# Batched row scatters and reordered LayerNorm statistics in an attention and mixture-of-experts layer

## The chip, the cores and the metric

The kernel runs on one core of a Trainium2 chip. Such a core has five engines, each with an instruction queue of its own that it works off in order: TensorE (PE, matrix products), VectorE (DVE), ScalarE (ACT), GpSimd (POOL) and SyncE (SP, which here issues most DMA transfers). The metric is the device time of one execution in microseconds (us), lower being better.

## The reference

The input x has 32 sequences of 256 tokens with 128 features, 8,192 tokens in all. Everything is float32.

```python
mod = (_silu(c) @ wmod).reshape(32, 6, 1, -1)          # sa, ca, ga, sb, cb, gb
h = _layernorm(x) * (1 + ca) + sa
x = x + ga * attn(h)                                   # gated linear scan
h = _layernorm(x) * (1 + cb) + sb
x = x + gb * ffn(h)                                    # 8 experts, top 2

def attn(x):
    g = sigmoid(x @ Wg.T + bg)
    a = sigmoid(x @ Wd.T + bd)
    v = x @ Wv.T + bv
    return scan(h_t = a_t * h_{t-1} + (1 - a_t) * v_t) * g

def ffn(x):
    probs = softmax(x @ gate_w.T + gate_b)
    topk_vals, topk_idx = top_k(probs, 2)
    h = relu(einsum('nd,edh->neh', x, w1) + b1)        # hidden size 512
    y = einsum('neh,eho->neo', h, w2) + b2
    return sum over the two chosen experts of topk_vals * y
```

## The kernel before

**Supertiles.** The tokens are taken in 16 supertiles of 512 (four tiles of 128, T = 4). Each supertile goes through four steps:

- `a_norm` (L312): first LayerNorm. VectorE's `bn_stats` (L280) and `bn_aggr` (L282) give mean and variance, `rsqrt` (L284 to L308) a reciprocal root in some ten small VectorE steps (for the first three supertiles with a power on GpSimd), ScalarE writes the normalised tiles (L324).
- `a_mix`: transposes px (L337), gated projections pz (L346), the scan on VectorE (L365, L366).
- `a_res`: transposes po back (L374), the residual (L376), the statistics of the second LayerNorm and its normalised tiles xm (L382, ScalarE).
- `a_route` (L385): transposes ph, logits pl (L397), the rows to be routed, rw (L402, ScalarE), top 2 of 8 on VectorE, ranks among the tokens of the same expert by small matmuls pq (L423, L425), and from these the row numbers pi (L439, VectorE). Then the weights of the two choices are added to rw (L444), and the token numbers by GpSimd (L445). Each supertile has 8 scatters (4 tiles, 2 choices, L447): GpSimd sends 128 rows each with an indirect DMA into a DRAM buffer `reg`, in which each expert has a region of its own.

**Blocks.** The rows in `reg` are worked off in 71 blocks of 256 rows of one expert. After supertiles 2 to 8, 10 and 12 (TAKE) and after the last, `table` (L471) works out from the running counts which blocks are certainly full, and puts the expert and first row of each into a small table tb. The tables hold blocks 0 to 4 (supertile 2), then four each up to block 28 (supertiles 3 to 8), 29 to 36 (10), 37 to 44 (12) and 45 to 70 (15). After the last supertile `fills` (L522) pads what is left of each region.

A block goes through `b_load` (SyncE reads expert and row from tb, L535 and L536, loads 256 rows xr, 130 KB, L538, and the expert's first-layer weights ww, 514 KB, L544; ww has five buffers, loads run four blocks ahead), `b_in` (transposes pbx, L551), `b_up` (three products p per part, L566 to L568; bias and relu to hh, L572 and L574), and `b_down` (bias matmul pby L584, products L587, weighted copy yt on ScalarE L591, eight buffers, and two scatters of result rows by GpSimd into DRAM, yd L593). The three are staggered: in one `b_step`, block i enters, block i-1 is in `b_up`, block i-2 in `b_down`. When all rows of a supertile are there, `c_load` (L600) and `c_add` (L610) sum its two results and the residual and write the output.

**Order.** A hand-written order (HEAD, L31) opens the program; after that each round t runs a_norm of supertile t, a_mix of t-1, a_res of t-2 and a_route of t-3, with a `b_step` after most of the steps as soon as more than two blocks are ready (L677 to L735). The program order, with priorities (AHEAD) for the later steps, decides each engine's queue order.

**How scatters are sent now.** `a_route` doesn't issue its 8 scatters: it puts them on a list (`sending`). `drip` (L461) takes one or two of the list at a time, after each step and each `b_step`, and gives each scatter a wait on a ScalarE instruction of the step or block just emitted (the activations remembered under "last"). Blocks of a new table lie in `held` until the last scatter of that table's supertile has been emitted, and only then join `blocks`. In `b_load` each xr load carries explicit waits on the last 16 scatters, and its value loads are kept behind the load of the block before it.

Two further places matter: rw (L401) and pi (L438) have three buffers each, and `late_constants` (L218), called after round 3, prepares constants of the final sum (among them sT3, the transformed rows mr and the selector sel, L227 to L240).

Of the kernel before, what the change touches and what calls it, by code (L numbers as in the profile page):

```python
# [15 lines left out]
AX = mybir.AxisListType  # L16
WAIT = mybir.DependencyInfo(mybir.DependencyClass.Sync, mybir.DependencyReason.DATA)

# [13 lines left out]

LATE = 3

XE = 3
# [19 lines left out]
def adaln_moe(ctx: ExitStack, tc: tile.TileContext, x, Wg, bg, Wv, bv, Wd, bd,  # L55
# [164 lines left out]
    def late_constants():  # L220
        nc.vector.tensor_copy(b2s[:, 0], b2r)
        nc.vector.tensor_tensor(b2s[:, 1], b2r, b2s[:, 0], op=ALU.subtract)
        for h in range(2):
            nc.sync.dma_start(b2w[h:h + 1].bitcast(F32), b2s[:, h].bitcast(F32))


        sT3 = cp.tile([P, 3, NB], F32, name="sT3")  # L227
        nc.vector.tensor_copy(sT3, sT.unsqueeze(1).to_broadcast([P, 3, NB]))
        pr = psa.tile([P, 512], F32, tag="pq", name="pr")
        nc.tensor.matmul(pr[:N3, :D], sT3.rearrange("p a b -> p (a b)"), wm[:, 5 * D:], start=True, stop=True)  # L230
        mr = cp.tile([N3, D], F32, name="mr")
        guarded(mr, pr[:N3, :D], [N3, D], 1.0, "gr")
        nc.vector.tensor_copy(mr3, mr)
        for i in (1, 2, 2):
            w = slice(i * NB, (i + 1) * NB)
            nc.vector.tensor_tensor(mr[w], mr[w], mr3[w], op=ALU.subtract)
            nc.vector.tensor_copy(mr3[w], mr[w])

        nc.vector.tensor_tensor(sel, ident[:N3, 0:NB], ident[:N3, NB:2 * NB], op=ALU.add)
        nc.vector.tensor_tensor(sel, sel, ident[:N3, 2 * NB:N3], op=ALU.add)  # L240
# [34 lines left out]

    def stats(mv, src, name):
        n = src.shape[1]
        st = wk.tile([P, T, 6], F32, tag=f"st{name[0]}", name=f"st{name}")
        for j in range(n):
            nc.vector.bn_stats(st[:, j], src[:, j])  # L280
        for j in range(n):
            nc.vector.bn_aggr(mv[:, j], st[:, j])  # L282
# [27 lines left out]
    ln1 = {}  # L310

    def a_norm(s):  # L312
        g = LN1G.get(s, 0)
        if g:
            mv = wk.tile([P, g * T, 2], F32, tag=f"mva{g}", name=f"mva{s}")
            for i in range(g):
                stats(mv[:, i * T:(i + 1) * T], xa[:, s + i], f"a{s + i}")
            y, r = rsqrt(mv, f"a{s}", s)
            for i in range(g):
                ln1[s + i] = (y[:, i * T:(i + 1) * T], r[:, i * T:(i + 1) * T])  # L320
        y, r = ln1[s]
        xn = wk.tile([P, T, D], F32, tag="xn", name=f"xn{s}")
        for j in range(T):
            last = nc.scalar.activation(xn[:, j], xa[:, s, j], AF.Identity, scale=y[:, j], bias=r[:, j])  # L324
        return dict(s=s, xn=xn, last=last)

# [6 lines left out]
    def a_mix(a):  # L333
# [10 lines left out]
        for i in (2, 1, 0):  # L344
# [3 lines left out]
            if i == 2:  # L348
                ta = wk.tile([P, ST], F32, tag="ta", name=f"ta{s}")
                nc.scalar.activation(ta, z, AF.Tanh, scale=0.5, bias=hb[:, 2:3])  # L350
                aa = wk.tile([P, ST], F32, tag="aa", name=f"aa{s}")
                nc.scalar.activation(aa, ta, AF.Copy, scale=0.5, bias=0.5)
                for q in range(BPS):
                    w = slice(q * S, (q + 1) * S)
                    b = s * BPS + q
                    nc.vector.tensor_scalar(ta[:, w], ta[:, w], ngq[:, b:b + 1], gq[:, b:b + 1], op0=ALU.mult, op1=ALU.add)
            elif i == 1:
                nc.vector.scalar_tensor_tensor(ta, z, bvc, ta, op0=ALU.add, op1=ALU.mult)
            else:
                tg = wk.tile([P, ST], F32, tag="tg", name=f"tg{s}")  # L360
                a["last"] = nc.scalar.activation(tg, z, AF.Tanh, scale=0.5, bias=hb[:, 0:1])  # L361
        hs = wk.tile([P, ST], F32, tag="hs", name=f"hs{s}")
# [6 lines left out]
    def a_res(a):  # L369
# [11 lines left out]
        for j in range(T):  # L381
            a["last"] = nc.scalar.activation(xn[:, j], xt[:, j], AF.Identity, scale=y[:, j], bias=r[:, j])  # L382
        a["xn"] = xn

    def a_route(a, base):  # L385
# [13 lines left out]
        for j in range(T):  # L399
            nc.tensor.transpose(pb[:, j * P:(j + 1) * P], hT[:, j * P:(j + 1) * P], ident)  # L400
        rw = wk.tile([P, T, K, RW], F32, tag="rw", name=f"rw{s}", bufs=3)  # L401
        a["last"] = nc.scalar.activation(rw[:, :, :, 0:D], pb.rearrange("p (t d) -> p t d", d=D).unsqueeze(2).to_broadcast([P, T, K, D]), AF.Copy)  # L402
        lg = wk.tile([P, T, E], F32, tag="lg", name=f"lg{s}")
# [33 lines left out]
        nc.vector.tensor_reduce(pf, oh, axis=AX.X, op=ALU.add)  # L437
        pi = wk.tile([P, T * K], I32, tag="pi", name=f"pi{s}", bufs=3)  # L438
        nc.vector.tensor_copy(pi, pf.rearrange("p t k -> p (t k)"))  # L439
        sm = wk.tile([P, T], F32, tag="sm", name=f"sm{s}")  # L440
# [4 lines left out]
        nc.gpsimd.tensor_copy(rw[:, :, :, D + 1].bitcast(I32), dst[:, s * T:(s + 1) * T])  # L445
        def send(j, k):
            w = nc.gpsimd.indirect_dma_start(  # L447
                out=reg, out_offset=bass.IndirectOffsetOnAxis(ap=pi[:, j * K + k:j * K + k + 1], axis=0),
                in_=rw[:, j, k], in_offset=None)
            into_reg(w.ins, "scat")  # L450
            return w.ins

        sending.extend((s, send, j, k) for j in range(T) for k in range(K))
        return rk[:, T]


    sending = []
    sent = []
    held = []

    def drip(n, behind):  # L461
        for _ in range(min(n, len(sending))):
            s, send, j, k = sending.pop(0)
            w = send(j, k)
            tc.add_manual_dep(w, behind.ins.name, WAIT, reason="pace of the rows on their way out")
            sent.append(w)
            if not sending or sending[0][0] != s:
                while held and held[0][0] <= s:
                    blocks.extend(held.pop(0)[1])

# [59 lines left out]

    loaded = []

    def b_load(n, tb, i):
        with tc.issue_after(loaded[-1].ins) if loaded else nullcontext():
            e = nc.sync.value_load(tb[i:i + 1, 0:1], min_val=0, max_val=E - 1)  # L535
            r = nc.sync.value_load(tb[i:i + 1, 1:2], min_val=0, max_val=E * CAP)  # L536
        xr = bk.tile([P, NJ, RW], F32, tag="xr", name=f"xr{n}", bufs=YTB + 6)
        w = nc.sync.dma_start(xr, reg[bass.ds(r, BLK)].rearrange("(t p) d -> p t d", p=P))  # L538
        tc.add_to_no_dep_group("rows", w.ins)
        for x in sent[-2 * K * T:]:  # L540
            tc.add_manual_dep(w.ins, x.name, WAIT, reason="its rows")
        ww = bk.tile([P, WW], F32, tag="ww", name=f"ww{n}", bufs=5)
        b = dict(n=n, xr=xr, ww=ww, tb=tb, i=i)
        loaded.append(nc.sync.dma_start(ww, wd[bass.ds(e, 1)].rearrange("o p f -> p (o f)")))  # L544
        return b
# [11 lines left out]
    def b_up(b):  # L557
        n, xs, ww = b["n"], b["xs"], b["ww"]
        hh = bk.tile([P, NH, BLK], F32, tag="hh", name=f"hh{n}")
        for k0 in range(0, NH, 2):  # L560
# [8 lines left out]
            for k in (k0, k0 + 1):  # L569
# [3 lines left out]
                else:  # L573
                    w = nc.scalar.activation(hh[:, k], p1[:, k - k0], AF.Relu, bias=bias)  # L574
                    b.setdefault("last", w)
        b["hh"] = hh
# [56 lines left out]
    def b_step():  # L633
# [12 lines left out]
        if i >= 1 and flow[i - 1]:  # L646
            b_up(flow[i - 1])
            drip(1 if alive else 2, flow[i - 1]["last"])
        if i >= 2 and flow[i - 2]:
# [7 lines left out]
    slot = 0  # L657
    alive = True

# [24 lines left out]
    for t, todo in enumerate(steps):  # L684
        def step3(s):
            nonlocal base, done
            with tc.high_priority(AHEAD[3] * (s >= EARLY)):
                base = a_route(st[s], base)
                if s in CLS:
# [3 lines left out]
                    counts.append(b)  # L693
                nb = len(blocks) + sum(len(x) for _, x in held)
                if s in TAKE:
                    n = full(s) - nb
                    tb, done = table(s, counts[:1] * (s > CUT) + [base], done, n, False)
                    held.append((s, [(tb, q, []) for q in range(n)]))
                elif s == NS - 1:
                    n = touched(s) - nb  # L700
                    tb, done = table(NS, counts, done, n, True)
                    fills(base)
                    rest = [(tb, q, []) for q in range(n)]
                    held.append((s, rest))
                    z = 0
                    for c in CLS:
                        u = max(E, touched(c) - nb) if c == CUT else touched(c) - nb
                        rest[u - 1][2].extend(range(z, c + 1))
                        z = c + 1
# [13 lines left out]
        for i, s in todo:  # L723
            (step0, step1, step2, step3)[i](s)
            drip(2 if t < len(steps) - NS or len(sending) > K * T else 1, st[s]["last"])
            between()
# [4 lines left out]
        if t == LATE:  # L731
            late_constants()
    alive = False
    while len(flow) < len(blocks) + 2 or ended or adding:
        b_step()  # L735
    assert not sending and not held

# [27 lines left out]
```

## Time and profile before

| what | value |
|---|---|
| median of 14 runs | 544.82 us (542.92 to 549.79) |
| profiled execution, whole | 545.21 us |
| its span | 543.4 us |
| PE busy | 440.2 us (81% of the span) |
| PE weight load busy | 368.0 us (68%) |
| VectorE busy | 283.3 us (52%) |
| ScalarE busy | 288.3 us (53%) |
| GpSimd busy | 292.5 us (54%) |
| mean granted clock of PE | 0.87 |

The profile is of one execution. Busy time of PE includes matmuls that run at a lower granted clock, so a busy PE is not one at its best. Further places of the trace that are of use below:

| what | when (us) |
|---|---|
| row numbers pi of supertiles 0, 1, 2, 3 written (start of L439) | 46.3, 59.9, 64.5, 89.6 |
| pi of supertiles 8, 12, 15 | 193.2, 283.5, 344.2 |
| supertile 0's eight scatters | 47.70 to 57.97 |
| last scatter of supertile 15 starts | 406.6 |
| first block's transposes | 100.4 |
| rows out for blocks 31, 36, 41, 46 (yt) | 349.2, 377.9, 409.2, 432.8 |
| last block's rows out | 530.5 |

Indirect DMAs on GpSimd take 0.95 to 1.5 us each (L447: 128, 981 ns on the mean; L593: 142, 998 ns), with 0.30 us between one and the next when nothing else holds them.

### The profile page before, as it was taken

Reading aid. Unit: us, or ns where it says so; the run is one execution under the profiler, and the core shown is the slowest. Engines: PE = TensorE matmul, PEld = TensorE weight load, DVE = VectorE, ACT = ScalarE, POOL = GpSimd, SP = SyncE. Lnnn points to the kernel's source line nnn. Section 1 sums busy time; section 2 is a strip of 40 time slices with the busy share of each in tenths; the row PEclk is TensorE's granted clock in tenths of the full one; section 3 lists DMA queues with packets and bytes.
Section 4 is the critical chain, followed back from the end, with each engine's and each line's share of the span. In section 5 each row is a group of like instructions: output and inputs, shape, how many; then the busy total and the mean of one; then the engine's idle time right before and its main releaser. Section 6 shows DMA issues by size and latency. Waiting matters only on the chain.

```text
span 543.4 us, 11399 instructions
## 1 busy us (share of the span) xinstructions
PE 440.2 (81%) x2810; PEld 368.0 (68%) x2810; DVE 283.3 (52%) x1511; ACT 288.3 (53%) x726; POOL 292.5 (54%) x322
## 2 busy tenths in 40 slices
PE   5868557698797899879969797895967999989990
PEld 3335315576786778658768686784966999979980
DVE  6899899476572765547556532311110221344364
ACT  4777445657573667646555553333323556655650
POOL 4436653445656656655566665565665255545451
PEclk9875675698797979898979996899889899999997
DMA  7993110647163644444442664566417777999974
GB/s 212 330 313 154 45 40 20 193 122 219 46 191 100 180 129 136 108 133 131 135 111 71 188 170 118 167 173 188 139 46 205 208 226 217 274 330 312 317 216 128
DMA packets 81845, 91.52 MB, mean 168 GB/s; under 512 B 8577, under 2 KB 66408, under 8 KB 81782
## 3 DMA queue, kind: packets, MB, share of 16 engines
q1 hardware_dynamic: 73024, 73.84, 47.4%
q0 software_dynamic: 8704, 16.94, 9.1%
q8 instruction: 26, 0.43, 0.3%
q14 instruction: 37, 0.30, 0.2%
q10 hardware_dynamic: 54, 0.02, 0.0%
HBM read 64.24 MB, written 27.43 MB: 169 GB/s over the span
## 4 chain that ended last, share of the span: by engine, by line
PE 52%; DVE 13%; issue 9%; another core or an unknown queue 9%; ACT 8%; DMA 5%; SPq 2%; POOL 1%; ACTq 0%; POOLq 0%; DVEq 0%
PE pby L587 22%; PE p L566 5%; PE p L568 5%; PE p L567 5%; PE pz L346 4%; PE pby L584 4%; PE pbx L551 3%; ACT yt L591 2%; DMA yk<-yd 2%; ACT hh L574 1%; PE pl L397 1%; DVE sta L280 1%; DVE hs L365 1%; DMA xa<-in_L_attn_x_dram 1%
## 5 line engine op out<-in xcount | busy, mean ns | idle before, releaser
L593 POOL DMA_INDIRECT yd<-yt,xr x142 | 141.7, 998 | 134.3 <-ACT yt L591 96.8
L447 POOL DMA_INDIRECT reg<-rw,pi x128 | 125.6, 981 | 76.8 <-issue 37.1
L587 PE MATMUL pby<-wr,hh 128*128 x1136 | 164.8, 302 | 0.8 <-issue 0.7
L587 PEld LDWEIGHTS pby<-wr,hh 128*128 128x128 f32 x1136 | 149.5, 211 | 10.4 <-issue 2.0
L574 ACT ACTIVATE hh<-p,ww 128x256 f32<-128x256 f32 x231 | 95.8, 479 | 36.9 <-issue 10.9
L591 ACT ACTIVATE yt<-pby,xr 128x128 f32<-128x128 f32 x142 | 44.9, 364 | 132.4 <-PE pby L587 60.1
L554 DVE TENSOR_TENSOR xs<-pbx,xs 128x256 fp32r<-128x256 f32 x71 | 29.9, 421 | 133.4 <-ACT xs L553 99.6
L566 PE MATMUL p<-xs,ww 128*128 128x256 f32 x284 | 91.7, 324 | 8.6 <-DVE hh L572 4.3
L567 PE MATMUL p<-xs,ww 128*128 128x256 f32 x284 | 83.0, 293 | 0.5 <-issue 0.4
L568 PE MATMUL p<-xs,ww 128*128 128x256 f32 x284 | 83.0, 293 | 0.0
L346 PE MATMUL pz<-h,wT 128*128 128x512 f32 x96 | 60.5, 752 | 5.8 <-ACT tg L361 3.3
L566 PEld LDWEIGHTS p<-xs,ww 128*128 128x128 f32 x284 | 57.1, 202 | 11.7 <-DVE hh L572 5.6
L567 PEld LDWEIGHTS p<-xs,ww 128*128 128x128 f32 x284 | 57.2, 201 | 2.2 <-issue 2.0
L584 PE MATMUL pby<-b2w,ones_r 2*128 x71 | 28.2, 397 | 35.2 <-ACT yt L591 33.3
L568 PEld LDWEIGHTS p<-xs,ww 128*128 128x128 f32 x284 | 56.5, 199 | 0.2 <-issue 0.2
L584 PEld LDWEIGHTS pby<-b2w,ones_r 2*128 2x128 f32 x71 | 13.6, 191 | 52.3 <-ACT yt L591 39.2
L572 DVE TENSOR_SCALAR hh<-p,ww 128x256 f32<-128x256 f32 x53 | 25.4, 479 | 22.4 <-ACT hh L574 17.6
L346 PEld LDWEIGHTS pz<-h,wT 128*128 128x128 f32 x96 | 20.2, 241 | 22.3 <-issue 9.4
L551 PE MATMUL pbx<-ident,xr 128*128 128x128 f32 x142 | 30.3, 298 | 4.1 <-DMA xr<-reg 3.2
L553 ACT ACTIVATE xs<-pbx 128x256 fp32r<-128x256 f32 x71 | 27.4, 386 | 10.0 <-PE pbx L551 3.8
L324 ACT ACTIVATE xn<-xa,nra,nya 128x128 f32<-128x128 f32 x64 | 26.5, 498 | 8.4 <-DVE nra L307 8.4
L382 ACT ACTIVATE xm<-xa,nrb,nyb 128x128 f32<-128x128 f32 x64 | 26.4, 483 | 6.2 <-DVE nyb L306 3.6
(181 smaller groups left out, 591.9 us busy)
## 6 DMA issues: line engine op xcount, KB each, us to landing
ww<-wd SPq DMA_DIRECT2D x71, 514.0 KB
xr<-reg SPq DMA_DIRECT2D x71, 130.0 KB
yk<-yd SPq DMA_DIRECT2D x30, 256.0 KB
wd<-wh SPq DMA_DIRECT2D x8, 514.0 KB
xa<-in_L_attn_x_dram SPq DMA_DIRECT2D x16, 256.0 KB
out_dram<-ot SPq DMA_DIRECT2D x15, 256.0 KB
yd<-yt,xr POOLq DMA_INDIRECT x142
w1s<-in_L_ffn_w_dram SPq DMA_DIRECT2D x8, 256.0 KB
```

The lines of the kernel that those rows point to most:

```text
L346: nc.tensor.matmul(z, wT[:, i], h1, start=True, stop=True)
L447: w = nc.gpsimd.indirect_dma_start(out=reg, out_offset=bass.IndirectOffsetOnAxis(ap=pi[:, j * K + k:j * K + k + 1], axis=0), in_=rw[:, j, ...
L551: nc.tensor.transpose(px[:, j * P:(j + 1) * P], xr[:, j, 0:D], ident)
L554: nc.vector.tensor_tensor(xs[:, 1], px, xs[:, 0], op=ALU.subtract)
L566: nc.tensor.matmul(z, hi, xs[:, 0], start=True, stop=False)
L567: nc.tensor.matmul(z, hi, xs[:, 1], start=False, stop=False)
L568: nc.tensor.matmul(z, lo, xs[:, 0], start=False, stop=True)
L574: w = nc.scalar.activation(hh[:, k], p1[:, k - k0], AF.Relu, bias=bias)
L584: nc.tensor.matmul(py.rearrange("p (j d) -> p j d", d=D), ones_r, b2t, start=True, stop=False)
L587: nc.tensor.matmul(py[:, j * D:(j + 1) * D], hh[:, k, j * P:(j + 1) * P], we[:, k * D:(k + 1) * D], start=False, stop=(j == NJ - 1 and k = ...
L591: nc.scalar.activation(yt[:, j], py[:, j * D:(j + 1) * D], AF.Copy, scale=xr[:, j, D:D + 1])
L593: w = nc.gpsimd.indirect_dma_start(out=yd, out_offset=bass.IndirectOffsetOnAxis(ap=xr[:, j, D + 1:D + 2].bitcast(I32), axis=0), in_=yt[:, ...
```

## The change

The eight scatters of a supertile are issued together at the end of `a_route`. The list, `drip`, `held` and the ScalarE instructions remembered for them are gone, and a table's blocks join `blocks` as soon as the table is emitted. The loads of rows lose their explicit waits on the 16 scatters (the dependence of the load on the scatters into `reg`, by the groups that `into_reg` declares, stays), and the value loads lose their order behind the load of the block before. rw and pi go back from three buffers to the pool's two. The first-LayerNorm `bn_stats` get an order (same engine, no semaphore) behind the pi copy of the supertile that was routed last when they are emitted: those of supertile 3 behind pi of 0, of 4 behind pi of 1, and so on. The second half of `late_constants` becomes `later_constants`, called after round 8.

```diff
-WAIT = mybir.DependencyInfo(mybir.DependencyClass.Sync, mybir.DependencyReason.DATA)
+ORDER = mybir.DependencyInfo(mybir.DependencyClass.NoSync, mybir.DependencyReason.DATA)
+LATER = 8
...
+    def later_constants():
         sT3 = cp.tile([P, 3, NB], F32, name="sT3")
...
-    def stats(mv, src, name):
+    def stats(mv, src, name, behind=None):
...
-            nc.vector.bn_stats(st[:, j], src[:, j])
+            w = nc.vector.bn_stats(st[:, j], src[:, j])
+            if behind:
+                tc.add_manual_dep(w.ins, behind.name, ORDER, reason="not ahead of the supertiles that route")
...
-                stats(mv[:, i * T:(i + 1) * T], xa[:, s + i], f"a{s + i}")
+                stats(mv[:, i * T:(i + 1) * T], xa[:, s + i], f"a{s + i}", placed[-1] if placed else None)
...
-        rw = wk.tile([P, T, K, RW], F32, tag="rw", name=f"rw{s}", bufs=3)
+        rw = wk.tile([P, T, K, RW], F32, tag="rw", name=f"rw{s}")
...
-        pi = wk.tile([P, T * K], I32, tag="pi", name=f"pi{s}", bufs=3)
-        nc.vector.tensor_copy(pi, pf.rearrange("p t k -> p (t k)"))
+        pi = wk.tile([P, T * K], I32, tag="pi", name=f"pi{s}")
+        placed.append(nc.vector.tensor_copy(pi, pf.rearrange("p t k -> p (t k)")).ins)
...
-        sending.extend((s, send, j, k) for j in range(T) for k in range(K))
+        for j in range(T):
+            for k in range(K):
+                w = nc.gpsimd.indirect_dma_start(
+                    out=reg, out_offset=bass.IndirectOffsetOnAxis(ap=pi[:, j * K + k:j * K + k + 1], axis=0),
+                    in_=rw[:, j, k], in_offset=None)
+                into_reg(w.ins, "scat")
...
-    def drip(n, behind):
-        for _ in range(min(n, len(sending))):
-            s, send, j, k = sending.pop(0)
-            w = send(j, k)
-            tc.add_manual_dep(w, behind.ins.name, WAIT, reason="pace of the rows on their way out")
-            sent.append(w)
-            if not sending or sending[0][0] != s:
-                while held and held[0][0] <= s:
-                    blocks.extend(held.pop(0)[1])
...
-        with tc.issue_after(loaded[-1].ins) if loaded else nullcontext():
-            e = nc.sync.value_load(tb[i:i + 1, 0:1], min_val=0, max_val=E - 1)
-            r = nc.sync.value_load(tb[i:i + 1, 1:2], min_val=0, max_val=E * CAP)
+        e = nc.sync.value_load(tb[i:i + 1, 0:1], min_val=0, max_val=E - 1)
+        r = nc.sync.value_load(tb[i:i + 1, 1:2], min_val=0, max_val=E * CAP)
...
-        for x in sent[-2 * K * T:]:
-            tc.add_manual_dep(w.ins, x.name, WAIT, reason="its rows")
...
-                    held.append((s, [(tb, q, []) for q in range(n)]))
+                    blocks.extend((tb, q, []) for q in range(n))
...
+        if t == LATER:
+            later_constants()
```

## The prediction

> **What bounds the kernel now.** I read the windows by stage first (boundaries: first block's transpose pbx at 100.4 us; last rank matmul pq of supertile 15 at 342.7; dense end from 434.6), then the chain of waits inside them, then the waits. Columns of a window: start and end, length, busy time and count on PE, PE weight load, VectorE (DVE), ScalarE (ACT) and GpSimd (POOL), granted clock, DMA share, GB/s.
>
> ```profile
> 0.00:100.40 100.40, 66.39 (x212) 37.61 (x213) 88.10 (x595) 58.39 (x120) 51.12 (x71) 0.72 0.50 154
> 100.40:342.70 242.30, 206.95 (x1352) 177.04 (x1353) 134.12 (x769) 139.85 (x354) 139.62 (x149) 0.88 0.48 140
> 342.70:434.60 91.90, 73.70 (x508) 67.30 (x507) 17.52 (x57) 34.99 (x99) 52.08 (x55) 0.91 0.55 159
> 434.60:530.20 95.60, 92.45 (x739) 85.78 (x739) 37.80 (x79) 54.43 (x153) 47.63 (x47) 1.00 0.90 270
> 530.20:543.40 13.20, 0.68 (x6) 0.23 (x4) 5.76 (x13) 0.62 (x2) 2.02 (x2) 0.70 0.43 123
> ```
>
> Only the fourth window is PE at its best: 24 blocks (47 to 70) in 95.6 us, 3.98 us a block. The first is VectorE's (88.1 of 100.4 us busy) and has no block in it at all. Why block 0 waits so long is in the chain:
>
> ```profile
> 92.97 0.95 POOL reg L447
> 93.93 0.30 issue
> 94.23 3.61 DMA reg<-rw,pi
> ...
> 98.14 2.19 DMA xr<-reg
> ...
> 100.40 0.69 PE pbx L551 x2
> ```
>
> Block 0 belongs to supertile 2's table. That supertile's eighth row scatter (L447) goes out at 94.23, lands 3.61 us later, and the block's rows take 2.19 us to load. The scatters are paced one or two at a time behind ScalarE instructions, and stood waiting for them (timeline of GpSimd; in brackets the idle time before and what ended it):
>
> ```profile
> 71.67 0.96 POOL L447 DMA_INDIRECT reg<-rw,pi  x1 [3.51 <-ACT xm L382]
> ...
> 87.46 0.98 POOL L447 DMA_INDIRECT reg<-rw,pi  x1 [6.48 <-ACT e L431]
> ```
>
> The waits say how the queues stand over the whole span: SyncE's loads wait for those scatters, GpSimd mostly waits for block results, ScalarE sometimes for something the profile can't name (us in all, times, longest).
>
> ```profile
> SPq L538 <- DMA reg<-rw,pi: 72.6, 15, 17.2
> SPq L544 <- DVE hh L572: 43.5, 20, 5.6
> ```
>
> ```profile
> POOL yd L593 <- ACT yt L591: 96.8, 54, 4.8
> ...
> ACT yt L591 <- remote: 39.9, 8, 6.2
> ```
>
> **Yardsticks.** A block costs 3.98 us. A supertile's routing on PE costs about 5.6 us (estimate): 16 transposes at the 0.11 us of pbx (0.22 for two in the full-clock chain) are 1.8; six L346 matmuls, four times as wide as a pby matmul (1.98 us for 16, 0.124 each), are 3.0; eight logit and five rank matmuls, small, some 0.8. Window two holds 31 blocks and parts of a 32nd, 31.5 (125.4 us), and by its matmuls about 10.2 supertiles' work (57 us): 182.4 us in 242.3, a pace of 0.753. Window three holds 257 pby matmuls, 16.06 blocks, 63.9 of 91.9 us: 28 us lost.
>
> **Part 1, statistics moved behind (and the later constants): first block earlier.** In the built order 96 fewer VectorE instructions stand ahead of pi0, the copy at L439 that frees supertile 0's scatters (150 against 246): 28 bn_stats, 20 bn_aggr, 45 small steps of the reciprocal root, 3 of the constants. From the VectorE timeline before it, four bn_stats take 0.86 us, four bn_aggr 0.37, a small step holds the engine 0.08: 28 x 0.215 = 6.0, 20 x 0.09 = 1.9, 48 x 0.08 = 3.8, together 11.7 us. VectorE was busy 26.2 of the 27.4 us before pi0 ended at 47.4, so most of it comes off: 0 to 11.7, taken 9, for pi0 then meets ScalarE's and PE's own chain. pi0 ends about 38. The moved work is not saved: it lies behind pi0 to pi2, where VectorE now has time while scatters go out; if VectorE were still late at pi2 (116 instructions fewer ahead), its 64.5 would simply hold.
>
> **Part 2, scatters at once.** Eight scatters take 8 x (0.96 + 0.30) = 10.1 us on GpSimd, as in the undisturbed run after 47.70. From 38.4: supertile 0 to 48.5, the two weight splits (L247, 1.28 each) now queued behind them to 51.1, supertile 1 to 61.2, supertile 2 to 71.3 (pi2 is needed by 61.2; with 116 instructions less, about 10 us, it comes near 55). Landing 2.1 to 3.61, taken 3, load 2.19: pbx0 at about 77. Bounds: 72 with all VectorE time gained, 90 if GpSimd is held by the splits and the powers as before. Gain 23 us. In the order, about one supertile's routing (5.6 us) less stands ahead of pbx0; it is due later.
>
> **Part 3, blocks released at once.** pq15 stands behind pby35 in place of pby30: about 36 blocks and 11.2 supertiles lie between pbx0 and pq15, 143.3 + 62.7 = 206 us dense; at 0.753 that is 274, pq15 at 351. Against that pace, bounds 0.70 (294) and 0.82 (251). Then 35 blocks x 3.98 = 139.3, a loss, and window five's 13.2. The loss was 28 us before. Four pieces of it, 4.13 + 2.87 + 5.83 + 6.25 = 19.1 in the chain, have no named cause ("another core or an unknown queue", ScalarE waiting on PE), and no edit removes them outright; the rest is pacing. Six blocks (24 us) stand between pq15 and block 45, whose path is 2 to 3 for the ranks, two yd scatters 2.6, batch 10.1, landing 3, load 2.2: 21, so covered. I take 10, between 0 and 28.
>
> ```profile
> 345.14 4.13 another core or an unknown queue
> ...
> 372.10 5.83 another core or an unknown queue
> ...
> 390.77 6.25 another core or an unknown queue
> ```
>
> **Part 4, waits added.** rw and pi have two buffers, so ScalarE's copy (L402) and pi wait for the scatters of the supertile two before: those are over about 15 us after their pi, and pi copies are 21.9 us apart (283.5 to 304.8 to 322.6 among others); nothing. If that cover went, each supertile would wait the difference, with VectorE's later work and the blocks' ScalarE work behind it. On GpSimd a batch stands in front of the yd scatters of a block: 10.1 us late at worst; yt has eight buffers, so ScalarE isn't stopped. GpSimd carries 10.1 + 3 x 2.56 = 17.8 us a supertile against 17.5 dense on PE, nearly level. On SyncE a waiting xr load now holds all ww loads behind it, as it did before; value loads and constants that change place cost under a microsecond.
>
> Sum: 77 + 274 + 139.3 + 10 + 13.2 = 513.5 of span, where the profiled run had 543.4. Around its span lie 1.8 us (545.21 in all; the median is 544.82, so no correction): **515**.
>
> The granted clock fits a saving that isn't proportional: sixteen pby matmuls took 3.71 us at 379.17, after a gap, and 1.98 at full clock. The Trainium skill, "TensorE: Matmul & The Clock Gate" (Part 1), says that half rate is the default and is left after about 3.4 us of sustained work. That speaks against one long wait in place of several short ones: by it ten long stalls would cost an estimated 10 x 1.7 = 17 us more; the rows here show the slow stretch after gaps, but not how short a gap is harmless.
>
> **Rivals.**
> A, start gain only: the whole 28 us of window three stay because their cause is not pacing. 544.8 - 23 + 5.6 for the routing due later = 527. For it: the unnamed 19.1. Against it: held blocks left PE waiting too (pby waits for yt 13.6 us there).
> B, more: at pace 0.82, no loss after pq15: 77 + 251 + 139.3 + 13.2 + 1.8 = 482. For it: SyncE's 72.6 us of waiting for scatters. Against: the unnamed waits go through window two as well.
> C, slower: the distance on PE from pq to its table's first block shrinks to 2 to 6 blocks, mostly 4 or 5 (5 to 12 before). The path over GpSimd in order is rank matmul to pi 5.8 (one late arrival like the 5.83), a yt wait 4.8, two yd 2.6, batch 10.1, landing 3.6, SyncE's wait for a ww buffer 5.6, load 2.2: 34.7 us. Cover: 15.9 + 5.6 = 21.5 dense, 28.5 at today's pace. The excess over it, 6.2, at eight tables, is 50 us: 565. It decides from 30 / 8 = 3.7 us of excess a table. For it: all these waits occur; against it, not all at once.
> D, the change doesn't bite: order and counts show that it does; what could be is that gains and new waits cancel, 545.
>
> **How the numbers follow.** 0.3% (1.6 us) is about what a measurement of this kernel tells from no change. The forecast, 498 to 526, has 0.46; A 0.18; B (to 497) 0.14; C 0.18; D 0.04. Faster 0.78, same 0.04, slower 0.18. The range that leaves out the ends of B and C: 484 to 552.
>
> **What would show it.** pi0 near 38, pbx0 at 72 to 90, L447 in unbroken rows of eight 1.27 us apart, pq15 between 330 and 370 with 35 blocks left, no SyncE wait of 17 us for reg. Wrong: pbx0 after 95, or PE's pbx (L551) waiting for xr more than 3 us at table after table, which is C; ScalarE's rw waiting for a scatter would be Part 4.

## The result

The changed kernel takes 587.44 us (median of 10 runs, 584.54 to 594.11) against 544.41 us before (47 runs): a ratio of 1.0803, 95% interval 1.0769 to 1.0838. It is slower by 8%; the forecast was 515 and faster.

The profile after, by the stages used before (boundaries: the first block's pbx at 89.6 us, the last routing until 421.5, the dense end from 442; columns as before: length, busy time and count on PE, PE weight load, VectorE, ScalarE, GpSimd, granted clock, DMA share, GB/s):

```profile
0.00:89.60 89.60, 47.38 (x163) 26.45 (x164) 61.65 (x336) 46.58 (x96) 46.88 (x65) 0.75 0.66 205
89.60:421.50 331.90, 248.38 (x1563) 207.45 (x1561) 166.75 (x1039) 163.75 (x410) 164.51 (x178) 0.83 0.35 108
421.50:442.00 20.50, 12.61 (x65) 11.47 (x65) 5.45 (x28) 5.05 (x15) 13.30 (x14) 0.67 0.30 94
442.00:577.50 135.50, 131.46 (x1019) 121.73 (x1018) 46.22 (x96) 74.81 (x209) 63.88 (x65) 0.98 0.82 250
577.50:590.80 13.30, 0.57 (x4) 0.23 (x4) 5.77 (x13) 0.32 (x2) 2.22 (x2) 0.63 0.39 113
```

The first block starts 10.8 us earlier (100.4 before). From there to the last rank matmul pq15 (at 412.2, from the PE timeline) the kernel needs 322.6 us where it needed 242.3, with 36 blocks in it in place of 31; from pq15 to the end 178.6 against 200.7. The sum, -10.8 + 80.3 - 22.1, is the 47.4 us by which the span grew; five blocks, some 20 us, have moved from behind pq15 to before it. The whole loss is in the stage in which routing and blocks run together.

What the queues waited for in it is not what the rivals named. SyncE no longer waits for the scatters, and PE waits for rows once, 0.5 us; ScalarE and VectorE wait for something the profile can't name ("remote": no matching instruction's recorded end lies within 1.5 us before the semaphore's update). In this stage the two wait so for 138.7 us where it was 34.3, four times as long; over the whole span, which these lines show, for 146.6 where it was 53.4 (total, times, longest):

```profile
POOL yd L576 <- ACT yt L574: 181.2, 54, 23.5
...
ACT yt L574 <- remote: 53.6, 9, 9.4
DVE xa L382 <- remote: 46.5, 7, 11.9
...
ACT hh L558 <- remote: 20.9, 6, 5.3
...
ACT ta L356 <- remote: 17.7, 5, 5.7
```

One period of it. The scatters of one supertile go out in one run with the result scatters before and behind them (GpSimd's timeline):

```profile
208.41 0.98 POOL L576 DMA_INDIRECT yd<-yt,xr  x1 [2.43 <-ACT yt L574]
...
211.45 0.96 POOL L454 DMA_INDIRECT reg<-rw,pi  x1 [0.79 <-issue]
212.72 0.96 POOL L454 DMA_INDIRECT reg<-rw,pi  x1 [0.30 <-issue]
...
220.31 0.96 POOL L454 DMA_INDIRECT reg<-rw,pi  x1 [0.30 <-issue]
...
222.86 0.98 POOL L576 DMA_INDIRECT yd<-yt,xr  x1 [0.30 <-issue]
```

In that time PE has done its part, but its readers don't start (PE, then VectorE, then ScalarE):

```profile
213.75 0.60 PE L380 MATMUL po<-ident,hs 128*128 128x128 f32 x4
214.18 1.88 PE L352 MATMUL pz<-h,wT 128*128 128x512 f32 x4
...
226.44 0.90 PE L395 MATMUL ph<-ident,xm 128*128 128x128 f32 x3 [6.07 <-DVE tb L499]
```

```profile
221.22 0.16 DVE L305 TENSOR_TENSOR nta<-nta,nva 128x4 f32<-128x4 f32 x1
225.69 0.69 DVE L382 TENSOR_TENSOR xa<-po,xa 128x512 f32<-128x512 f32 x1 [4.31 <-remote]
```

```profile
220.06 0.47 ACT L558 ACTIVATE hh<-p,ww 128x256 f32<-128x256 f32 x1 [3.96 <-remote]
223.57 0.84 ACT L558 ACTIVATE hh<-p,ww 128x256 f32<-128x256 f32 x2 [3.04 <-remote]
225.73 0.69 ACT L356 ACTIVATE ta<-pz,hb 128x512 f32<-128x512 f32 x1 [1.32 <-remote]
```

The transposes po are recorded as ended by 214.35; xa, which needs them and nothing later of PE, starts at 225.69, 11.3 us later, 1.8 us after the run of scatters has ended. Then PE, which stood for 6 us, goes on with ph of the supertile before, whose buffer xa had to read first (po and ph share one). I call the time from the recorded end of the PE instruction that a reader waits for to the reader's start a hand-off. Counted over the trace, some 85 of 463 hand-offs are later than 4 us after the change and 45 later than 8 us; before, 60 of 451 and none (bias matmuls, which nothing reads by themselves, and final sums left out; a reader's engine can have been busy with other work in between). Before, GpSimd's runs (scatters under 1.5 us apart) had at most eight scatters, and the unnamed stalls of 4 to 6 us that the prediction showed lie beside runs of five and six. The one beside the stall at 372.10, six scatters, begins and ends so:

```profile
369.22 0.96 POOL L447 DMA_INDIRECT reg<-rw,pi  x1 [2.03 <-ACT hh L574]
...
375.59 0.96 POOL L447 DMA_INDIRECT reg<-rw,pi  x1 [0.30 <-issue]
```

After, there are thirteen runs of ten or twelve, from 99.9 us on, and beside each of them the latest hand-off is 6.8 to 13.4 us late; beside the first three runs, of seven and eight, none is later than 2.5 us.

The Trainium skill, "Perfetto Trace Analysis" (Tensor Engine Instruction), says that the end shown for a matmul is computed, and that the semaphore update is pushed only once PSUM has acknowledged the bytes and then still has to spread. The trace, which keeps the times of the semaphores' updates, narrows it down. Nine updates of PE's semaphore are due between 212.28 and 220.37 us and nine are recorded behind them, the fifth, that of po, at 225.67, 0.02 us before xa. Of 21 hand-offs over 8 us whose reader's engine stood idle, 19 start within 0.03 us of such an update. So the reader isn't what is late, but the update; no run here tells whether it leaves PE late or spreads late. Within runs of five and more scatters the trace has 62 updates of PE where 148 instructions owe one, outside them 377 for 389.

### The profile page after: what moved, and what is told of

It reads as the page before. It is cut to its first block, busy times and chain, and to the rows that moved or that the text cites. A ratio compares the mean times of both kernels' runs of the same rounds, so it can differ in the third digit from the quotient of the medians.

```text
span 590.8 us, 11357 instructions
## 1 busy us (share of the span) xinstructions
PE 440.4 (75%) x2810; PEld 367.3 (62%) x2810; DVE 285.8 (48%) x1511; ACT 290.5 (49%) x726; POOL 290.8 (49%) x322
## 4 chain that ended last, share of the span: by engine, by line
PE 43%; DVE 17%; issue 13%; another core or an unknown queue 13%; ACT 9%; DMA 3%; SPq 1%; POOL 0%; ACTq 0%; DVEq 0%; POOLq 0%
PE pby L570 17%; PE p L550 4%; PE p L552 4%; PE p L551 4%; PE pz L352 3%; PE pby L567 3%; ACT xn L330 2%; PE pbx L535 2%; ACT hh L558 2%; ACT yt L574 2%; PE pl L403 2%; PE ph L395 1%; DVE hs L371 1%; DVE sta L282 1%
## 5 line engine op out<-in xcount | busy, mean ns | idle before, releaser
L454 POOL DMA_INDIRECT reg<-rw,pi x128 | 123.6, 966 | 55.9 <-issue 35.0
L550 PE MATMUL p<-xs,ww 128*128 128x256 f32 x284 | 91.9, 325 | 15.1 <-DVE tb L499 7.9
L552 PE MATMUL p<-xs,ww 128*128 128x256 f32 x284 | 84.3, 297 | 3.0 <-issue 3.0
L551 PE MATMUL p<-xs,ww 128*128 128x256 f32 x284 | 84.8, 299 | 1.5 <-issue 1.5
L538 DVE TENSOR_TENSOR xs<-pbx,xs 128x256 fp32r<-128x256 f32 x71 | 29.9, 421 | 112.8 <-ACT xs L537 57.7
L550 PEld LDWEIGHTS p<-xs,ww 128*128 128x128 f32 x284 | 58.3, 206 | 19.0 <-DVE tb L499 8.1
L552 PEld LDWEIGHTS p<-xs,ww 128*128 128x128 f32 x284 | 58.1, 205 | 4.2 <-issue 4.2
L551 PEld LDWEIGHTS p<-xs,ww 128*128 128x128 f32 x284 | 58.7, 207 | 2.4 <-issue 2.4
L395 PE MATMUL ph<-ident,xm 128*128 128x128 f32 x64 | 16.0, 380 | 26.2 <-DVE xa L382 19.0
L382 DVE TENSOR_TENSOR xa<-po,xa 128x512 f32<-128x512 f32 x16 | 11.0, 690 | 49.0 <-remote 46.5
```

The lines of the kernel that those rows point to most:

```text
L454: w = nc.gpsimd.indirect_dma_start(out=reg, out_offset=bass.IndirectOffsetOnAxis(ap=pi[:, j * K + k:j * K + k + 1], axis=0), in_=rw[:, j, ...
L550: nc.tensor.matmul(z, hi, xs[:, 0], start=True, stop=False)
L551: nc.tensor.matmul(z, hi, xs[:, 1], start=False, stop=False)
L552: nc.tensor.matmul(z, lo, xs[:, 0], start=False, stop=True)
```

## The experiments

Theories when they began: R, long unbroken runs of scatters hold up hand-offs; S, the statistics ordered behind pi now stand in the loop from one supertile to the next; Q, blocks released early stand in PE's order too close to their routing.

**All scatters at once, alone (e1_once; f1_once, g_once, h_once the same kernel).** Blocks are released at the place where they were.

```diff
-        sending.extend((s, send, j, k) for j in range(T) for k in range(K))
+        sending.extend((s, send(j, k)) for j in range(T) for k in range(K))
...
-            s, send, j, k = sending.pop(0)
-            w = send(j, k)
-            tc.add_manual_dep(w, behind.ins.name, WAIT, reason="pace of the rows on their way out")
+            s, w = sending.pop(0)
```

> The kernel before with one part of the change: the eight scatters of a supertile go out together from a_route; blocks are released where they were, the order of statistics, the buffers and the constants stay. Theory R (long unbroken runs of scatters on GpSimd hold up what the other engines hand to each other; 10 to 12 in a row after, at most 8 before): most of the loss shows, 570 to 595 us, and PE's results reach ScalarE or VectorE over 10 us late beside each run. Theory S (the statistics, ordered behind pi, stand in the loop): no loss, 535 to 548. Theory Q (blocks released early stand in PE's order too close to the routing of their rows): no loss, 535 to 548.

Measured: 467.84 us against 476.58, ratio 0.984 (0.975 to 0.992). Not only no loss: the kernel before itself took 476.58 on this chip where the record has 544. No theory had said that, and from here each result is told with its own runs of the kernel before.

**The order of the statistics, alone (e2_order)**, with the later constants; scatters paced as before.

```diff
-            nc.vector.bn_stats(st[:, j], src[:, j])
+            w = nc.vector.bn_stats(st[:, j], src[:, j])
+            if behind:
+                tc.add_manual_dep(w.ins, behind.name, ORDER, reason="not ahead of the supertiles that route")
```

> The kernel before with the order of the statistics behind pi and the later constants alone; scatters paced, blocks held as before. Theory R: no loss, 525 to 546, less by what an earlier first block brings. Theory S: most of the loss, 570 to 595. Theory Q: 525 to 546.

Measured: 481.51 against 476.58, ratio 1.011 (1.004 to 1.018). On this chip the order costs 1% when the scatters stay paced: its first block comes at 103.9 us, no earlier, since the last scatters of supertile 2 still wait for their ScalarE instructions.

**The change without that order (e3_no_order; f3_no_order, g_no_order).**

```diff
-                stats(mv[:, i * T:(i + 1) * T], xa[:, s + i], f"a{s + i}", placed[-1] if placed else None)
+                stats(mv[:, i * T:(i + 1) * T], xa[:, s + i], f"a{s + i}")
```

> The changed kernel without the order of the statistics (all else as changed). Theory R: the loss stays, 580 to 600. Theory S: the loss goes, 505 to 535. Theory Q: 580 to 600.

Measured: 464.52 against 476.58, ratio 0.975 (0.967 to 0.982).

**Result scatters in runs of eight (e5_runs_of_8; f5_, g_, i_runs_of_8).** From block 46 on, the yd scatters of four blocks are issued behind the fourth.

```diff
             b_down(flow[i - 2])
+            held_yd.append(flow[i - 2])
+            n = flow[i - 2]["n"]
+            if n < GROUP_FROM or n % 4 == 0 or flow[i - 2]["ends"]:
+                while held_yd:
+                    b_send(held_yd.pop(0))
```

> The kernel before, with the scatters of result rows of blocks 46 to 70 issued in runs of eight behind every fourth block instead of two behind each; their number and sizes stay. PE is dense there and no routing runs. Theory R: each of about six runs costs 4 to 8 us, 568 to 592 in all, and the dense end shows PE's results arriving late beside the runs. Theories S and Q, and a version of R in which only the scatters of routed rows do it: 543 to 549, the last group's scatters alone being later.

Measured: 476.33 against 476.58, ratio 0.999 (0.996 to 1.003). The edit didn't do what it says: GpSimd took the scatters as each block's results came, and its profile (i_runs_of_8, below) has no run over two in the dense end. It tells nothing on R; being the kernel before in effect, it lends its profile for the other chips below.

**Both kernels again (p_before, p_after)**, to have them on one chip with a profile.

> The kernel before, unchanged, for its profile beside the runs of this study, in which it takes 476.6 us where the record has 544. If the difference is what Theory R names (other engines' results reaching their readers late beside runs of scatters), the waits of ScalarE and VectorE for an unnamed source (39.9 us for the result rows in the record) are gone here, and the stage up to the last rank matmul is the one that is shorter. If instead all stages are shorter by one ratio (0.875), it is a clock or a memory and says nothing on the change.

> The changed kernel, unchanged, on the same chip as the kernel before here. Theory R: without late results the change brings what it brought in the two single-part runs, 462 to 472 us against 476.6, and no unnamed wait above 10 us in all. Theory S or Q: the loss of 8% stays, 510 to 520.

Measured on another chip: 545.38 for the kernel before (548.96 in the seven runs beside it), 589.88 for the changed one, ratio 1.077 (1.068 to 1.087). So the chips differ, not the kernels. Seven chips were met: on four the kernel before takes 474.7 to 476.6 us (the faster kind below), on three 544.1 to 549.0 (the slower kind), with nothing between. The stages aren't shorter by one ratio: to the first block 101.8 us in p_before and 98.6 in g_runs_of_8 (in effect the same kernel, on the faster kind), from there to pq15 240.3 and 192.1, to the end 201.6 and 185.5. The traces differ in one more thing: on the slower kind they hold 71 to 77% of the semaphore updates that PE's, VectorE's and ScalarE's instructions owe, on the faster kind 99%; whether the others weren't recorded or came merged isn't shown.

**The same again, to meet either kind (f1_once, f3_no_order, f5_runs_of_8) and the scatters spaced (f4_spaced).**

```diff
+                nc.gpsimd.memset(gap, 0.0)
                 w = nc.gpsimd.indirect_dma_start(
```

> All scatters of a supertile at once, nothing else, a second time, since chips differ: one ran the kernel before in 476.6 us without late results, two in 545 with them. Where the kernel before takes 545: Theory R (unbroken runs of scatters hold up the other engines' hand-offs there) 565 to 590, with unnamed waits above 100 us; Theory S (statistics in the loop) and Theory Q (order of blocks) 535 to 548. Where it takes 476: 468 again.

> The changed kernel without the order of the statistics, a second time. Where the kernel before takes 545: Theory R and Theory Q 575 to 600, Theory S 505 to 540. Where it takes 476: 464.5 again.

> The kernel before with result scatters of blocks 46 to 70 in runs of eight, a second time. Where the kernel before takes 545: Theory R 560 to 592, with late results of PE beside the runs in the dense end; Theories S and Q, and R for scatters of routed rows alone, 543 to 550. Where it takes 476: 476 again.

> The changed kernel with a clearing of a 128x512 tile on GpSimd, whose output nothing reads, before each of the eight scatters, so that they are further apart. Where the kernel before takes 545: Theory R 550 to 580, less than the changed kernel's 588 although GpSimd has more to do; Theories S and Q 588 to 605. Where it takes 476: 470 to 490, GpSimd being longer at each supertile.

Measured, the kernel before at 475.26: 469.88 (0.989, 0.980 to 0.998), 465.51 (0.981, 0.973 to 0.989), 476.48 (1.004, 1.000 to 1.007), and spaced 474.17 (0.998, 0.994 to 1.002). The clearings of the last were taken out of place in GpSimd's order: whole batches of eight still went out 1.27 us apart (at 113.15 to 122.02 us, for one), so it says nothing on the distance, only that this kernel with eight clearings a supertile has no gain.

**The whole change on that kind of chip (g_after, with g_once, g_no_order, g_runs_of_8).**

> The changed kernel unchanged. Where the kernel before takes 475: Theory R (loss only where results are handed over late) 460 to 472; Theories S and Q 505 to 520. Where it takes 545: 588 again, all theories.

> All scatters of a supertile at once, blocks released where they were. Where the kernel before takes 545: Theory R 565 to 590, S and Q 535 to 548. Where it takes 475: 468 to 470, as measured twice.

> The changed kernel without the order of the statistics. Where the kernel before takes 545: Theories R and Q 575 to 600, Theory S 505 to 540. Where it takes 475: 465, as measured twice.

> Result scatters of blocks 46 to 70 in runs of eight. Where the kernel before takes 545: Theory R 560 to 592, others and R for routed rows alone 543 to 550. Where it takes 475: 476.

Measured, the kernel before at 475.96: the changed kernel **459.87, ratio 0.966 (0.958 to 0.975)**; 468.48 (0.985), 465.05 (0.980), 476.68 (1.003). On this kind the change is a gain of 3.4%; nothing in it costs what the record shows, so S and Q, which don't depend on the chip, can't carry the loss. The profile of the changed kernel there, the first two stages:

```profile
0.00:80.20 80.20, 49.67 (x164) 27.45 (x164) 60.74 (x345) 47.42 (x98) 47.13 (x65) 0.79 0.63 190
80.20:298.00 217.80, 209.80 (x1555) 183.53 (x1555) 165.02 (x1029) 163.06 (x406) 155.79 (x166) 0.97 0.55 173
```

The same work that took 322.6 us takes 217.8. VectorE's, ScalarE's and GpSimd's busy time hardly differ from the record's in the same stage (166.2, 162.0 and 159.2 us); PE's 209.8 against 246.4 fits the clock, 0.97 against 0.83 (246.4 x 0.83 / 0.97 = 210.8, an estimate).

**All scatters at once, on the slower kind (h_once).**

> All scatters of a supertile at once, blocks released where they were. Where the kernel before takes 545: Theory R 565 to 590, S and Q 535 to 548. Where it takes 475: 468 to 470, as measured three times.

Measured: 596.85 against 547.17, ratio 1.091 (1.081 to 1.101). This one part makes the whole loss; R's range ends 7 us below it. Its unnamed waits are 118.9 us in all, these two the largest; e1_once has none.

```profile
ACT yt L589 <- remote: 59.5, 6, 11.3
...
DVE xa L376 <- remote: 31.7, 3, 12.9
```

The same instructions on two chips, from the first block to pq15:

```profile
117.30:405.70 288.40, 217.16 (x1344) 182.28 (x1344) 135.68 (x760) 138.43 (x342) 147.17 (x158) 0.81 0.40 117
```

```profile
100.80:282.20 181.40, 179.75 (x1342) 156.93 (x1343) 138.42 (x764) 140.84 (x347) 133.98 (x143) 0.97 0.63 181
```

The first is h_once, the second e1_once. Where they part can be seen on VectorE, in a reciprocal root of the first LayerNorm. From 60 to 65.7 us h_once and g_once run alike within 0.1 us; GpSimd's scatters of supertiles 1 and 2 go out 1.27 us apart in both, from about 60 to 80 us. First h_once:

```profile
66.09 0.16 DVE L300 TENSOR_TENSOR nta<-nya 128x4 f32<-128x4 f32 x1
...
68.87 0.16 DVE L301 TENSOR_TENSOR nta<-nta,nva 128x4 f32<-128x4 f32 x1 [0.54 <-DVE nyb L306]
...
71.05 0.16 DVE L302 SCALAR_TENSOR_TENSOR nta<-nta 128x4 f32<-128x4 f32 x1 [0.55 <-DVE nrb L307]
...
75.31 0.16 DVE L303 SCALAR_TENSOR_TENSOR nya<-nta,nya 128x4 f32<-128x4 f32 x1 [1.26 <-DVE g L513]
...
80.29 0.16 DVE L304 TENSOR_TENSOR nta<-nya 128x4 f32<-128x4 f32 x1 [1.22 <-issue]
```

and g_once, the same five:

```profile
65.74 0.15 DVE L300 TENSOR_TENSOR nta<-nya 128x4 f32<-128x4 f32 x1
...
66.02 0.15 DVE L301 TENSOR_TENSOR nta<-nta,nva 128x4 f32<-128x4 f32 x1
...
66.39 0.15 DVE L302 SCALAR_TENSOR_TENSOR nta<-nta 128x4 f32<-128x4 f32 x1
...
66.78 0.15 DVE L303 SCALAR_TENSOR_TENSOR nya<-nta,nya 128x4 f32<-128x4 f32 x1
66.99 0.15 DVE L304 TENSOR_TENSOR nta<-nya 128x4 f32<-128x4 f32 x1
```

14.2 us against 1.25. Each instruction takes its 0.15 us in both; what is longer is the idle time before it, and what it waits for is VectorE's own earlier result. In runs of four and more scatters, from the third on, 16 of 155 such self-waits exceed 0.3 us in h_once and none of 520 in e1_once, which gets more than three times as many of them done within its runs.

**Does the distance decide (i_gaps), and do result scatters do it too (i_runs_of_8)?** i_gaps is h_once with a clearing of 128x512 on GpSimd between each two scatters, this time held in its place.

```diff
         def send(j, k):
+            g = nc.gpsimd.memset(gap, 0.0)
+            if last_sent:
+                tc.add_manual_dep(g.ins, last_sent[-1].name, ORDER, reason="after the scatter before")
             w = nc.gpsimd.indirect_dma_start(
...
             into_reg(w.ins, "scat")
+            tc.add_manual_dep(w.ins, g.ins.name, ORDER, reason="before the next scatter")
+            last_sent.append(w.ins)
```

> Result scatters of blocks 46 to 70 in runs of eight. Where the kernel before takes 545: Theory R in general (any scatters in a row) 560 to 592, with late results of PE beside the runs in the dense end; R for the scatters of routed rows alone 543 to 550. Where it takes 475: 476, as measured three times.

> All scatters of a supertile at once, as in the run before, with a clearing of a 128x512 tile on GpSimd (some 0.55 us, its output unread) held between each two, so that they are 1.8 us apart and the result scatters of blocks fall between them. Where the kernel before takes 545: Theory R 555 to 585, below the 597 without gaps, though GpSimd has 70 us more to do; if the number of scatters alone mattered, 597 to 620. Where it takes 475: 480 to 520, GpSimd having 22 us a supertile against 17 on PE.

Measured, the kernel before at 544.12: i_runs_of_8 547.27 (1.006, 1.002 to 1.010; void as said), i_gaps **541.30, ratio 0.993 (0.988 to 0.998)**, 55 us less than h_once, with GpSimd busy for 70 us more (360.2 us against 290.5). The clearing keeps them apart, result scatters come between, and no run is over four:

```profile
205.74 0.97 POOL L454 DMA_INDIRECT reg<-rw,pi  x1 [0.17 <-issue]
206.70 0.55 POOL L451 MEMSET gap<- 128x512 f32 x1
207.41 0.96 POOL L454 DMA_INDIRECT reg<-rw,pi  x1 [0.16 <-issue]
208.68 0.99 POOL L600 DMA_INDIRECT yd<-yt,xr  x1 [0.30 <-issue]
```

R's range (555 to 585) lies above that. Unnamed waits are down to 13.1 us, hand-offs over 4 us to 17 of 441, over 8 us to none (66 and 53 of 443 in h_once). To pq15:

```profile
108.80:310.40 201.60, 179.50 (x1263) 154.12 (x1262) 133.24 (x717) 129.46 (x326) 160.78 (x200) 0.95 0.50 145
```

201.6 us for 29 blocks, where h_once took 288.4 for 31, at a granted clock of 0.95. The gaps' price comes later: 227.7 us from pq15 to the end (201.6 in p_before): 42 blocks are left then in place of 40, and the last scatter goes out 77.3 us after pq15 in place of 66.2. Distance and length of a run change together here, so which of the two counts isn't shown.

**Gaps, and result scatters truly in rows (j_gaps_runs)**, each held by a wait on its group's last result.

> Two things in one kernel, read apart by stage: up to the end of routing the kernel of the gaps (541 against 544 on a chip of the slower kind), and from block 46 on result scatters truly in runs of eight, each held to the last result of its group by a wait. Where the kernel before takes 545: if any scatters in a row do it, about six runs with PE's results 4 to 12 us late, dense end 20 to 50 us longer, 560 to 590 in all; if only those of routed rows, or only with VectorE and ScalarE busy, the dense end stays at its 95 us and the total at 538 to 550. Where it takes 475: the gaps' price on such a chip, 470 to 500, the dense end within 3 us of before.

Measured: it met a chip of the faster kind: 532.00 against 474.67, ratio 1.121 (1.116 to 1.126). The stages are those of i_gaps (190.9 and 229.0 us), so there the two together cost 12% and bring nothing; 470 to 500 us was expected. Only the first two groups stand as rows in the profile (six and eight scatters); later ones come in smaller pieces. Between the two chips the same idea differs by 9 us (541 and 532) where the unspaced kernel differs by 129 (597 and 468). Whether result scatters in rows hold up hand-offs too, on the kind of chip where others do, stays open: no run put the two together.

## Why the prediction failed, by its steps

- **Part 1 held.** pi0 ended at 40.3 us (38 said, 47.4 before).
- **Part 2 held on GpSimd only.** The first eight scatters ended at 51.3 (48.5), the 24th at 74.8 (71.3), the first load of rows was issued at 76.6. But pbx0 came at 89.6, not 77: VectorE crept through those scatters (PE stood from 60.2 to 69.6 for the scan's result), and PE had routing ahead of pbx0 in its order. On the faster kind it was 80.2.
- **Part 3 is the step that failed: "at 0.753 that is 274, pq15 at 351", with bounds of 0.70 and 0.82.** Measured: 322.6 us, a pace of 206 / 322.6 = 0.64, and 36 blocks, as counted. What took its place are the late hand-offs, up to 13.4 us, beside runs of ten and twelve. The pace of before was itself a product of the pacing: runs of at most eight scatters and stalls of 4 to 6 us. The prediction saw those stalls, wrote that they "have no named cause" and that "no edit removes them outright", and let them stand as a constant, although the change rewrites the one queue beside which all of them lie. Laying GpSimd's timeline beside the four pieces it quoted would have shown runs of five and six scatters at each.
- **Part 4** counted a batch as ten microseconds of GpSimd. That is right for GpSimd (1.27 us a scatter on all chips). The two-buffer wait cost nothing on record, 2.4 us in p_after and 4.4 in g_after (rw 2.0, pi 2.4). It isn't always nothing: without the order of the statistics ScalarE stood for rw once for 13.9 us (e3_no_order) and 13.0 (g_no_order). The pi copies named lie 21.3 and 17.8 us apart, not 21.9.
- **After pq15**: 178.6 us for 35 blocks, against 139.3 + 10 + 13.2 = 162.5 said; only two blocks were done from pq15 to 442, so about 22 of it are lost in that stretch (29.8 less two blocks), beside the last two batches.
- **The rule on the clock** was priced at 17 us. The clock in the routing stage fell to 0.83 from 0.88, but behind the stalls: on the faster kind, with the same order and no stalls, it is 0.97, and on the slower kind with the gaps 0.95 (i_gaps). So it follows the stalls here.
- **Rivals.** C was on the right side (565) by luck, its mechanism didn't occur: blocks waited 0.5 us for rows in all. B's pace (0.82 and more) is what the faster kind of chip shows: 206 / 217.8 = 0.946, 459.9 us, where that chip's kernel before is at 476. So the parts that the forecast counted do bring 16 us there, less than the 30 said. The pace there is 0.95 before as well (182.4 dense in 192.1 us, g_runs_of_8), so there was little of it to gain.

What is shown: the scatters at once alone lose 9% on one kind of chip and gain 1 to 2% on the other; spacing them takes the loss away (one kernel on one chip). Beside the long runs PE's semaphore updates are late. What stays open is by what, and why only on some chips. Every run here comes with the profiler's span and clock, none was taken without recording, and the slower kind is the one whose records have gaps; whether the recording takes part in the loss is untested. The record's own chips are not known, but its 544 us, its unnamed waits and its gaps (72% of the updates recorded before, 76% after) are those of the slower kind.

No version was measured that beats both kernels on both kinds; the change without the order of the statistics ran on the faster kind alone. The changed kernel is the best measured on the faster kind (459.87), the one with gaps on the slower (541.30, 0.7% under before).

## What to carry to other kernels

A wait that the profile can't name is not a constant: lay every engine's timeline beside such stalls before keeping their pace in a sum, above all that of the queue that the change rewrites. Indirect DMAs back to back on GpSimd can, on some chips, delay what other engines hand to each other, and pacing that looks like idle time may be what prevents it; measure such a change on more than one chip. And see in the profile that an experiment did what its edit says: three of these didn't, or did so in part.

## What the hardware showed unexpectedly

- Trainium2 chips differ by 13% in this kernel (475 and 545 us) at equal times of the single instructions: a scatter has 0.96 us, a pby matmul 275 ns, a scan half 0.67 to 0.68 us on both kinds (medians).
- On the slower kind a run of ten to twelve scatters at 1.27 us made PE's results up to 14.1 us late for ScalarE and VectorE (p_after), and VectorE's own results 0.5 to 1.3 us late for itself in most steps of the root above (h_once). Paced, the latest was 6.7 us on record; on the faster kind, with runs of up to 71 scatters (e1_once), none was over 3.2.
- It isn't every run: in h_once the first eight scatters, 47.2 to 57.7 us, held nothing up, and the creeping began at 65.5, some five scatters into the next run.
- The Trainium skill, "SBUF — State Buffer" (Who interferes with whom), has a lock on SBUF ports that VectorE and GpSimd share, and says that PE and ScalarE never wait on anyone for ports. The lock could touch VectorE alone; here PE's results reach ScalarE up to 14.1 us late beside the scatters, and the same program on another chip shows neither delay, so that rule doesn't account for it.
